# Layer 1's last denominators in two more even stretches, and layer 3's mean-times-scale moved from VectorE to GpSimd

## The chip, the cores and the metric

The kernel runs on one core of one Trainium2 chip. The metric is the device time of one execution in microseconds, as the median of several runs. Engines are named as in the profile: PE is TensorE's matmul, PEld its weight load, DVE is VectorE, ACT is ScalarE, POOL is GpSimd, SP is SyncE (here a queue that issues transfers).

## The reference

Four graph layers follow each other, each of the form `x = layernorm(x + layer(x, adj))`, on 2708 rows of 256 features with a 2708 x 2708 adjacency matrix. Two of them matter here.

```
# layer 1, per head of 4 (64 features each)
h    = (x @ W).reshape(n, heads, head_dim)
e    = leaky_relu(src[:, :, None] + dst.T[None, :, :])
attn = softmax(where(adj > 0, e, NEG_INF), axis=-1)
out  = einsum('nhm,mhd->nhd', attn, h)           # then a layer norm
# layer 3
h = features @ neigh_W.T
h = adj @ h / (adj.sum(axis=1) + 1)
z = concatenate([features, h], axis=-1) @ lin_W.T
out = layernorm(x + z)                           # (y - mean) * (var + eps) ** -0.5
```

In layer 1 the kernel never forms the softmax: it sums unnormalised weights times `h` (the sums), sums the weights themselves (the denominators), and divides at the end.

## The kernel before

The 2708 rows are 22 tiles of up to 128. In layer 1 the outputs are worked off in three groups of two spans of tiles: the spans are 4, 4, 4, 4, 3 and 3 tiles, so two groups have 512 + 512 output rows and the last has 384 + 276 = 660 (the last tile has 20 rows). For each group the loop runs over two pairs of heads (`q` of 0 and 1) and, within a pair, over the 22 source tiles (`c`). A turn of `c` does this:

- DVE makes two weight tiles `p`, one for each head of the pair, of 128 x 1024 or, in the last group, 128 x 660 (line 835). Five `p` buffers rotate.
- PE adds into the sums: `heads` (line 817) runs four matmuls, for each span (`cols`) and each of the two heads, with 64 columns of weights each. The two heads of one span stand in different columns of the array.
- PE adds into the denominators: `totals` (line 826) runs four matmuls, again for each span and head, with 32 columns of weights each. The four stand in four different column groups, number `2 * (s ^ q) + i`, and all write the one PSUM tile `den`.

`heads` and `totals` change their order from turn to turn, so two `totals` and then two `heads` stand together. Between turns, `step` puts in pieces of the group before: transposes of its sums and denominators (lines 694, 695), its normalisation on DVE, ACT and POOL (`layer1_end`, lines 671 to 744), and, with `q` of 1, the transposes and products of the next layer's logits (lines 756, 773). At the end of each `q`, ACT copies the sums (line 848) and the denominators (line 852) from PSUM into `dens`, one tile per span, which the next group's `layer1_end` transposes. The last group's `layer1_end` runs beside the start of layer 2.

In layer 3 the product `adj @ h` is formed with fewer products by the two halves of the rows (`seven`, line 328) in three units, whose results are turned back by PE (`rows3`, line 1387) tile by tile, and the two tiles of `last3`, numbers 19 and 20, get plain products of 22 matmuls (line 1428). The last unit's turning back stands between the matmuls of tiles 19 and 20. For every tile `row3` runs: DVE scales and adds the row part (line 1368), then `moments` takes mean and variance on DVE (lines 172, 174, 176) and raises to the power -0.5 on POOL (line 177). The rest of the normalisation is put off: `ended` holds the tile, and `flush`, called in the `row3` of the next tile behind its `moments`, works it off: DVE forms `-mean * rs` (line 1361), ACT applies scale and bias to the 128 x 256 tile (line 1362), and the tile is written out (line 1363) from the ACT queue where its number is odd, from SP where it is even. SP's queue also issues nearly all loads of the adjacency matrix. The order on each engine is set by a planner that places instructions, not by the order of the text: it puts line 1361 of a tile ahead of the next tile's line 1368 where it expects the power to be done.

After the last write the program ends in a conditional (line 1654) that skips the variant for signed inputs.

Of the kernel before, what the change touches and what calls it, by code (L numbers as in the profile page):

```python
# [14 lines left out]
AF = mybir.ActivationFunctionType  # L15
ALU = mybir.AluOpType
# [3 lines left out]
P = 128  # L20
# [7 lines left out]
def kernel(  # L28
# [24 lines left out]
    nc = tc.nc  # L53
# [9 lines left out]
    CT = 32  # L63
# [18 lines left out]
    last3 = [t for t in range(NT) if min(P, N - t * P) == P][-2:]  # L82
# [6 lines left out]
    def sz(i):  # L89
        return min(P, N - i * P)  # L90

    def width(lo, hi):
        return min(hi * P, N) - lo * P
# [110 lines left out]
    def load_strip(pool, t):  # L204
        s = pool.tile([P, NT, P], F32, tag="strip", name="strip", bufs=2)
        nc.sync.dma_start(s, adj_t[t])
        return s
# [28 lines left out]
    def gru_load(pool, bih, bhh):  # L236

        raw = pool.tile([P, 2, 3 * FC], F32, tag="braw", name="braw", bufs=2)
        for i, src in enumerate((bih, bhh)):
            nc.sync.dma_start(raw[:, i], src.rearrange("(c p) -> p c", p=P))  # L240
        return raw
# [162 lines left out]
    if True:  # L404
# [12 lines left out]
        if True:  # L417
            def load_fall(dst, g, queue):
                at, w = spans[g][0] * P, width(*spans[g])
                off = at - spans[g - g % 2][0] * P  # L420
                queue.dma_start(dst[:, :, off : off + w], bcast_rows(fall_d, at, w))
# [34 lines left out]
            with pool("l0", 2) as l0:  # L456
# [48 lines left out]
                with pool("prep", side="right") as prep:  # L505
# [24 lines left out]
                    with tc.issue_after(landed.ins):  # L530
# [9 lines left out]
                        bias = [gru_load(prep, *ab) for ab in ((e_bih, e_bhh), (n_bih, n_bhh))]  # L540
# [64 lines left out]
                    t = ahead + 1  # L605
                    s = load_strip(l0, t)
# [21 lines left out]
                for t in range(ahead + 2, NT - 1):  # L628
                    s = load_strip(l0, t)
# [7 lines left out]
                t = NT - 1  # L637
                s = load_strip(l0, t)
# [22 lines left out]
            if True:  # L661
# [123 lines left out]
                dens = [keepr.tile([P, W], F32, name=f"den{s}") for s in range(2)]  # L785
                for g in range(0, len(spans), 2):
                    segs = spans[g : g + 2]
                    at, w = segs[0][0] * P, width(segs[0][0], segs[-1][1])
                    if g >= 4:
                        falls.append(fallp.tile([P, H, 2 * W], F32, tag="fall_b", name="fall_b"))  # L790
                        for i in range(len(segs)):
                            load_fall(falls[-1], g + i, nc.sync)
                    cols = [(lo * P - at, width(lo, hi)) for lo, hi in segs]
                    sums, steps, halves = [], [itertools.chain(*rest)] if g == 0 else [], []

                    def step(c):
                        for s in list(steps):
                            if next(s, s) is s:
                                steps.remove(s)

                        if q == 0 and c % 5 == 1 and len(halves) < len(ended):
                            halves.append(layer1_end(l1, ended[len(halves)]))
                            next(halves[-1])
                            steps.append(itertools.islice(halves[-1], 2))

                        if q == 1 and c % 5 == 0 and c // 5 < len(halves):
                            steps.append(itertools.chain(halves[c // 5], [None], layer1_logits(ended[c // 5])))
                            next(steps[-1])

                    for q in range(H // 2):  # L810
                        den = ps_acc.tile([P, W], F32, tag="acc", name="den")
                        acc = [ps_acc.tile([P, W], F32, tag="acc", name="acc") for _ in segs]

                        def heads(c, ps, flags):
                            for s, (p0, ws) in enumerate(cols):
                                for i in (1, 0):
                                    nc.tensor.matmul(  # L817
                                        acc[s][i * HD : (i + 1) * HD, :ws], hs[c][:, 2 * q + i, :HD],
                                        ps[i][:, p0 : p0 + ws], **flags,
                                    )  # L820

                        def totals(c, ps, flags):
                            for s, (p0, ws) in enumerate(cols):
                                for i in (1, 0):
                                    j = (2 * (s ^ q) + i) * CT
                                    nc.tensor.matmul(  # L826
                                        den[j : j + CT, :ws], hs[c][:, 2 * q + i, HD + 1 - CT :],
                                        ps[i][:, p0 : p0 + ws], **flags,
                                    )

                        for c in range(NT):
                            ps = []
                            for i in range(2):
                                p = l1.tile([P, 2 * W], F32, tag="p", name="p", bufs=5)
                                nc.vector.scalar_tensor_tensor(  # L835
                                    p[:, :w], falls[g // 2][:, 2 * q + i, :w], rise[:, c, 2 * q + i : 2 * q + i + 1],
                                    mask[:, c, at : at + w], ALU.max, ALU.mult,
                                )
                                ps.append(p)

                            for part in (heads, totals)[:: -1 if c % 2 == 0 else 1]:
                                part(c, ps, dict(start=(c == 0), stop=(c == NT - 1)))
                                if part is (totals, heads)[c % 2]:
                                    step(c)
                        got = []
                        for s, (p0, ws) in enumerate(cols):
                            sb = keepr.tile([P, W], F32, tag=f"sum{q}{s}", name=f"sum{q}{s}")
                            nc.scalar.copy(sb[:, :ws], acc[s][:, :ws])  # L848
                            got.append(sb)
                        for s, (p0, ws) in enumerate(cols):  # L850
                            two = slice(2 * (s ^ q) * CT, 2 * ((s ^ q) + 1) * CT)
                            nc.scalar.copy(dens[s][two, :ws], den[two, :ws])
                        sums.append(got)
                    for a in steps:
                        for _ in a:
                            pass
                    ended = [(t, s, sums, dens, t - segs[0][0]) for s, (lo, hi) in enumerate(segs) for t in range(lo, hi)]
                    ended = [ended[i : i + 2] for i in range(0, len(ended), 2)]
# [24 lines left out]
                for i in range(SPLITS):  # L883
                    part = u_parts[:, :, i * K : (i + 1) * K]
# [7 lines left out]
                for t in range(NT):  # L892
                    for b, acc in zip(banks, pus):
                        w = width(*spans[b[0]])
# [56 lines left out]
                def band_tile(nm):  # L951
                    return tail.tile([P, NT, BANDS, K], F32, tag=nm, name=nm, bufs=1)
# [7 lines left out]
                d, q, keep_q = band_tile("d"), band_tile("q"), band_tile("keep_q")  # L960
# [6 lines left out]
                for i in range(SPLITS):  # L967
                    part = q_parts[:, :, i * B : (i + 1) * B].rearrange("p t (b k) -> p t b k", k=K)
# [8 lines left out]
                for g in range(0, len(spans), 2):  # L977
                    two, w = range(g, g + 2), width(*spans[g])
# [16 lines left out]
                shift, den = tail.tile([P, NT, K], F32, name="shift", bufs=1), tail.tile([P, NT, K], F32, name="den", bufs=1)  # L995
# [23 lines left out]
                for lo in range(0, NT, 4):  # L1019
                    hi = min(lo + 4, NT)  # L1020
                    at, w = lo * P, width(lo, hi)
                    pt = ps_t.tile([P, 4, P], F32, tag="tr", name="pst")
                    for t in range(lo, hi):
                        n = sz(t)
# [80 lines left out]
    with (  # L1105
# [250 lines left out]
        def flush():  # L1356

            while ended:
                t, o, mean, rs = ended.pop()
                n = sz(t)  # L1360
                nc.vector.scalar_tensor_tensor(mean, mean, -1.0, rs, ALU.mult, ALU.mult)  # L1361
                nc.scalar.activation(o[:n], o[:n], AF.Identity, scale=rs, bias=mean)  # L1362
                (nc.scalar if t % 2 else nc.sync).dma_start(out[t * P : t * P + n, :], o[:n])

        def row3(t, o, acc):
# [51 lines left out]
        for t, tag in zip(last3, ("m1", "m26")):  # L1417
            o = nleft.tile([P, F], F32, tag="y", name="y", bufs=3)
# [3 lines left out]
            for lo in range(0, NT, per):  # L1422
                hi = min(lo + per, NT)
                s = nright.tile([P, 2, 2, W], F32, tag="p", name="p", bufs=3).rearrange("p i h w -> p (i h w)")
                s = s[:, : (hi - lo) * P].rearrange("p (c n) -> p c n", n=P)
# [275 lines left out]
```

## Time and profile before

| | |
|---|---|
| median of 3 runs | 1865.03 us (1864.9 to 1866.25) |
| profiled execution, its own time | 1865.35 us |
| its span | 1863.6 us |
| PE busy | 1832.7 us (98%) |
| DVE busy | 1280.9 us (69%) |
| ACT busy | 699.3 us (38%) |
| POOL busy | 266.4 us (14%) |
| last group of layer 1 | 498.2 to 590.5 us |
| layer 3's last unit turned back, and its end | 1835.9 to 1856.5 us |

Times in the profile count from the start of the span. PE works nearly all the time, so a change is worth something where it shortens what PE does, where it takes away a wait of PE's, or behind PE's last matmul, where other engines finish alone. fp32 matmuls appear as two records each. Lines of the profile are lines of the kernel before.

### The profile page before, as it was taken

What the parts mean: (1) busy time and instruction counts of PE and PEld (TensorE: products, weight loads), DVE (VectorE), ACT (ScalarE), POOL (GpSimd) and SP (SyncE); (2) the same over time, 40 slices, a digit from 0 to 9 for tenths busy, and PEclk for the clock granted to TensorE, in tenths of its full rate; (3) what the DMA queues carried; (4) which work ended last, traced back from release to release, by engine and by line L of the source; (5) the groups of instructions that cost most, each with busy time, mean ns of one, the idle gap of its engine ahead of it and who ended that gap; (6) DMA issues with size and microseconds to landing.
All of it is one profiled execution on the core that took longest, in us unless ns stands there. A gap on an engine that the chain in (4) does not pass through costs nothing. (4 is left out here: it accounts for less than half of the span.)

```text
span 1863.6 us, 23088 instructions
## 1 busy us (share of the span) xinstructions
PE 1832.7 (98%) x7526; PEld 1035.4 (56%) x7530; DVE 1280.9 (69%) x2263; ACT 699.3 (38%) x1442; POOL 266.4 (14%) x427
## 2 busy tenths in 40 slices
PE   9999999999999999999999999999999999999997
PEld 7788832233345887887444444444445556654555
DVE  5344489999897664754568888776887768844664
ACT  3544410033144203111546655555665556321011
POOL 1211220001012411000002000111200302111111
PEclk9999999999999999999999999999999999999999
DMA  8344410100002667754647666454554545634764
GB/s 298 133 148 151 168 30 1 30 1 12 12 7 71 144 144 186 182 130 114 182 131 207 176 174 171 123 159 114 165 151 121 135 106 141 167 106 116 203 163 121
DMA packets 435101, 237.32 MB, mean 127 GB/s; under 512 B 184363, under 2 KB 422348, under 8 KB 432540
## 3 DMA queue, kind: packets, MB, share of 16 engines
q1 hardware_dynamic: 422414, 208.66, 41.4%
q0 software_dynamic: 8208, 22.59, 3.9%
q10 hardware_dynamic: 4350, 4.50, 0.7%
q8 instruction: 62, 1.02, 0.2%
q14 instruction: 67, 0.55, 0.1%
HBM read 223.00 MB, written 12.66 MB: 126 GB/s over the span
## 5 line engine op out<-in xcount | busy, mean ns | idle before, releaser
L835 DVE SCALAR_TENSOR_TENSOR p<-fall_b,rise,mask 128x1024 f32<-128x1024 f32 (+1 forms) x264 | 293.9, 1156 | 32.5 <-PE den L826 16.7
L1328 ACT ACTIVATE p<-st,e_neg 128x1024 f32<-128x1024 f32 (+1 forms) x198 | 197.3, 1040 | 193.9 <-PE m L328 190.1
L328 PE MATMUL m<-s,xq 128*128 128x512 f32 (+3 forms) x660 | 230.1, 467 | 0.0
L817 PE MATMUL acc<-p,h 128*64 128x512 f32 (+2 forms) x1056 | 214.5, 548 | 0.2 <-ACT sum L848 0.2
L328 PE MATMUL m<-p,xq 128*128 128x512 f32 (+1 forms) x396 | 183.0, 544 | 0.1
L215 PE MATMUL acc<-turn,strip 128*128 128x257 f32 x792 | 181.8, 379 | 0.0
L1331 ACT ACTIVATE p<-p 128x1024 f32<-128x1024 f32 (+1 forms) x198 | 178.8, 942 | 0.2
L315 DVE TENSOR_TENSOR s<-p 128x512 f32<-128x512 f32 (+3 forms) x132 | 81.5, 618 | 136.6 <-PE m L328 112.7
L328 PE MATMUL m<-p,x 128*128 128x512 f32 (+1 forms) x396 | 167.7, 542 | 0.3 <-DVE supt L345 0.3
L328 PEld LDWEIGHTS m<-s,xq 128*128 128x128 f32 x660 | 124.5, 190 | 76.3 <-issue 59.2
L1332 DVE TENSOR_TENSOR p<-p,blk 128x1024 f32<-128x1024 f32 (+1 forms) x132 | 142.8, 1101 | 33.6 <-ACT p L1331 23.1
L215 PEld LDWEIGHTS acc<-turn,strip 128*128 128x128 f32 x792 | 147.2, 190 | 20.3
L817 PEld LDWEIGHTS acc<-p,h 128*64 128x64 f32 x1056 | 69.8, 136 | 138.2 <-issue 128.6
L328 PE MATMUL m<-s,x 128*128 128x512 f32 (+3 forms) x330 | 127.2, 467 | 0.0
L826 PE MATMUL den<-p,h 128*32 128x512 f32 (+2 forms) x1056 | 117.8, 548 | 0.0
L328 PEld LDWEIGHTS m<-p,xq 128*128 128x128 f32 x396 | 74.6, 190 | 76.9 <-issue 61.3
L328 PEld LDWEIGHTS m<-p,x 128*128 128x128 f32 x396 | 74.8, 190 | 75.5 <-issue 61.1
L474 ACT ACTIVATE below<-strip 128x384 bf16<-128x384 f32 x132 | 78.4, 594 | 68.4 <-DMA strip<-in_adj_t_dram 65.0
L316 DVE TENSOR_TENSOR p<-p 128x512 f32<-128x512 f32 (+3 forms) x132 | 82.3, 624 | 2.3
L328 PEld LDWEIGHTS m<-s,x 128*128 128x128 f32 x330 | 62.0, 190 | 39.2 <-issue 34.6
L318 DVE TENSOR_TENSOR s<-p,s 128x512 f32<-128x512 f32 (+3 forms) x132 | 81.2, 615 | 1.9
L286 POOL TENSOR_TENSOR blk<-blk,offdiag 128x128 f32<-128x128 f32 (+3 forms) x50 | 28.2, 566 | 376.0 <-DMA blk<-in_adj_t_dram 359.2
(288 smaller groups left out, 2591.9 us busy)
## 6 DMA issues: line engine op xcount, KB each, us to landing
strip<-in_adj_t_dram SPq DMA_DIRECT2D x19, 1408.0 KB, 6.0
blk<-in_adj_t_dram SPq DMA_DIRECT2D x88, 256.0 KB, 3.4
blk<-in_adj_t_dram SPq DMA_DIRECT2D x88, 192.0 KB, 4.1
pa<-in_adj_t_dram SPq DMA_DIRECT2D x110, 128.0 KB, 2.8
turn<-in_adj_t_dram SPq DMA_DIRECT2D x44, 256.0 KB, 3.1
blk<-in_adj_t_dram SPq DMA_DIRECT2D x88, 128.0 KB, 2.7
p<-in_adj_t_dram SPq DMA_DIRECT2D x88, 128.0 KB, 2.7
turn<-in_adj_t_dram SPq DMA_DIRECT2D x44, 192.0 KB, 3.1
```

The source lines that it names most:

```text
L215: at = nc.tensor.matmul(acc, s[:, c, :n], rhs(c), start=(c == 0), stop=(c == NT - 1))
L315: nc.vector.tensor_tensor(s1, a21, a22, ALU.add)
L316: nc.vector.tensor_tensor(a21, a21, a11, ALU.subtract)
L318: nc.vector.tensor_tensor(s4, a12, s2, ALU.subtract)
L328: nc.tensor.matmul(dst[:, :w], lt, rt, start=start and not (one_bank and i), stop=stop and not (one_bank and i in (1, 2, 5)))
L474: nc.scalar.activation(below[:, : (hi - lo) * P], s[:, lo:hi].rearrange("p c n -> p (c n)"), AF.Relu, scale=-1.0, accum_out=negative[:, BE ...
L817: nc.tensor.matmul(acc[s][i * HD : (i + 1) * HD, :ws], hs[c][:, 2 * q + i, :HD], ps[i][:, p0 : p0 + ws], **flags,)
L826: nc.tensor.matmul(den[j : j + CT, :ws], hs[c][:, 2 * q + i, HD + 1 - CT :], ps[i][:, p0 : p0 + ws], **flags,)
L835: nc.vector.scalar_tensor_tensor(p[:, :w], falls[g // 2][:, 2 * q + i, :w], rise[:, c, 2 * q + i : 2 * q + i + 1], mask[:, c, at : at + w] ...
L1328: nc.scalar.activation(p[:, :, :w], st_k[:, :, :w], AF.Relu, scale=-1.0, bias=e_neg[:, at, k : k + 1])
L1331: nc.scalar.activation(p[:, :, :w], p[:, :, :w], AF.Exp, scale=-1.0)
L1332: nc.vector.tensor_tensor(p[:, :, :w], p[:, :, :w], blk[:, i, :, :w], ALU.mult)
```

## The change

In layer 1, the denominators of a group are no longer split at the border of its spans but at `cut`, the middle of the group's rows rounded to a multiple of 64 and not behind the border. A group of 1024 rows is still split 512 + 512. The last group's 660 rows are split 320 + 340, where it was 384 + 276. The copies into `dens` keep their targets: the first span's 384 rows now come from two column groups, 320 and 64 rows, the second span's 276 from one. So ACT makes three copies at the end of each `q` of the last group, where it made two. The sums keep the spans.

In layer 3, `-mean * rs` moves from DVE to POOL, as one tensor_scalar on the same 128 x 1 columns, and for tile 20, the last, both that and ACT's normalisation are replaced by one DVE instruction on the 128 x 256 tile.

```diff
                     cols = [(lo * P - at, width(lo, hi)) for lo, hi in segs]
+                    cut = min(cols[1][0], (w // 2 + P // 4) // (P // 2) * (P // 2))
+                    halves_at = [(0, cut), (cut, w - cut)]
...
                         def totals(c, ps, flags):
-                            for s, (p0, ws) in enumerate(cols):
+                            for s, (p0, ws) in enumerate(halves_at):
                                 for i in (1, 0):
                                     j = (2 * (s ^ q) + i) * CT
                                     nc.tensor.matmul(
...
                             two = slice(2 * (s ^ q) * CT, 2 * ((s ^ q) + 1) * CT)
-                            nc.scalar.copy(dens[s][two, :ws], den[two, :ws])
+                            for i, (a, n) in enumerate(halves_at):
+                                lo, hi = max(p0, a), min(p0 + ws, a + n)
+                                if lo < hi:
+                                    part = slice(2 * (i ^ q) * CT, 2 * ((i ^ q) + 1) * CT)
+                                    nc.scalar.copy(dens[s][two, lo - p0 : hi - p0], den[part, lo - a : hi - a])
...
                 t, o, mean, rs = ended.pop()
                 n = sz(t)
-                nc.vector.scalar_tensor_tensor(mean, mean, -1.0, rs, ALU.mult, ALU.mult)
-                nc.scalar.activation(o[:n], o[:n], AF.Identity, scale=rs, bias=mean)
+                if t == last3[-1]:
+                    nc.vector.tensor_scalar(o[:n], o[:n], mean, rs, ALU.subtract, ALU.mult)
+                else:
+                    nc.gpsimd.tensor_scalar(mean, mean, rs, -1.0, ALU.mult, ALU.mult)
+                    nc.scalar.activation(o[:n], o[:n], AF.Identity, scale=rs, bias=mean)
                 (nc.scalar if t % 2 else nc.sync).dma_start(out[t * P : t * P + n, :], o[:n])
```

The planner then orders anew. PE's order stays the same throughout. DVE's and ACT's order changes inside layer 1's last group, where some of `layer1_end`'s instructions move from the first `q` into the second, and in layer 3 from the first turned tiles on. On SP, three writes of finished tiles in layer 3 move ahead by one load each.

## The prediction

> **What bounds the kernel now.** I read the page first, for which engine is full; then busy time by stretches around the two edited places; then the timeline of PE in layer 1; last the timeline of the end.
>
> ```profile
> PE 1832.7 (98%) x7526; PEld 1035.4 (56%) x7530; DVE 1280.9 (69%) x2263; ACT 699.3 (38%) x1442; POOL 266.4 (14%) x427
> ```
>
> PE is busy for 1832.7 of 1863.6 us, so matmul time that is saved counts unless another engine takes over. The two `q` of layer 1's last group, by stretches (columns: length, then busy us and instructions of PE, PEld, DVE, ACT, POOL, then clock, DMA share, GB/s):
>
> ```profile
> 498.20:544.50 46.30, 46.07 (x388) 21.04 (x388) 44.55 (x86) 24.26 (x126) 6.61 (x7) 1.00 0.00 1
> 544.50:590.50 46.00, 46.00 (x386) 22.41 (x382) 35.82 (x49) 9.39 (x28) 8.60 (x19) 1.00 0.08 23
> ```
>
> PE is full in both. In the first `q` DVE is nearly full too, 44.55 of 46.3 us: the place where a faster PE could meet DVE. In the second DVE has 10 us to spare. Now PE's timeline (start, us, then the instruction; x16 is two turns of `c`), of a full group and of the last:
>
> ```profile
> 325.80 3.65 PE L817 MATMUL acc<-p,h 128*64 128x512 f32 x16
> 329.38 1.92 PE L826 MATMUL den<-p,h 128*32 128x512 f32 x16
> 331.24 3.65 PE L817 MATMUL acc<-p,h 128*64 128x512 f32 x16
> ...
> 523.37 2.44 PE L817 MATMUL acc<-p,h 128*64 128x384 f32 x16
> 525.74 1.49 PE L826 MATMUL den<-p,h 128*32 128x384 f32 x16
> 527.16 2.44 PE L817 MATMUL acc<-p,h 128*64 128x384 f32 x16
> ```
>
> From start to start, two turns of sums take 3.58 us for 512 + 512 rows and 2.37 for 384 + 276: they follow the total, 1.67 ns a row and turn. Two turns of denominators take 1.86 us with 512 and 512 and 1.42 with 384 and 276, a ratio of 0.763. The longer stretches stand as 0.75, the totals as 0.645. So the denominators follow the longer stretch. The end, in the timeline of all engines (the bracket is the idle time before, and what ended it):
>
> ```profile
> 1846.81 4.48 PE L1428 MATMUL m<-turn,p 128*128 128x256 f32 x20
> ...
> 1851.43 0.16 DVE L1361 SCALAR_TENSOR_TENSOR bn_mv<-bn_mv,bn_rs 128x1 f32<-128x1 f32 x1 [0.71 <-POOL bn_rs L177]
> 1851.52 0.47 DVE L1368 SCALAR_TENSOR_TENSOR o<-m,rdeg,o 20x256 f32<-20x256 f32 x1
> ...
> 1853.54 0.15 DVE L1361 SCALAR_TENSOR_TENSOR bn_mv<-bn_mv,bn_rs 20x1 f32<-20x1 f32 x1 [0.71 <-POOL bn_rs L177]
> 1853.62 0.47 DVE L1368 SCALAR_TENSOR_TENSOR y<-m,rdeg,y 128x256 f32<-128x256 f32 x1
> ...
> 1855.09 0.54 POOL L177 TENSOR_TENSOR bn_rs<-bn_rs,neg_half 128x1 f32<-128x1 f32 x1 [1.59 <-DVE bn_rs L176]
> 1855.67 0.16 DVE L1361 SCALAR_TENSOR_TENSOR bn_mv<-bn_mv,bn_rs 128x1 f32<-128x1 f32 x1 [0.72 <-POOL bn_rs L177]
> 1855.86 0.60 ACT L1362 ACTIVATE y<-y,bn_mv,bn_rs 128x256 f32<-128x256 f32 x1 [1.54 <-DVE bn_mv L1361]
> 1856.49 0.33 SPq L1363 DMA_DIRECT2D out_dram<-y  x1
> ```
>
> PE's last matmul ends at 1846.81 + 4.48 = 1851.29, but tile 20's line 1368 starts at 1853.62. DVE is late: line 1361 of each tile stands ahead of the next tile's line 1368 and waits 0.71 us for POOL. DVE's starts of line 1368 lie 2.15 us apart (1849.37, 1851.52, 1853.62), while PE turns a tile back every 1.52 us.
>
> **What the Trainium skill says.** "TensorEngine Tiling (Array Packing)", Key Properties: tiles work independently, and different ones can load weights and multiply in parallel. The 0.763 above agrees. "GPSIMD Engine Reference", section 3.1, has a two-input elementwise operation about twice as slow on GpSimd as on VectorE; the trace has no such multiply on one column, only the power, 0.54 us. "DMA: Bandwidth & Descriptors", Anatomy of one DMA, puts some 2 us of fixed cost on a transfer; the writes of line 1363 land after a median of 2.2 us, and nothing here changes that.
>
> **The change, part by part.**
>
> *Denominators on PE.* The longer stretch falls from 384 to 340 rows, for 44 turns (22 tiles, two `q`), 22 pairs. By the slope of the two measured pairs, (1.86 - 1.42) / 128 x 44 = 0.151 us a pair. But 340 and 320 are nearly even, like 512 and 512, whose pair has 0.147 us on top of its rows (1.854 - 4 x 512 x 0.000833 us, two passes a turn), against 0.134 with 384 and 276. With that a pair takes 1.133 + 0.147 = 1.280, a gain of 0.134. I take the lower one: 22 x 0.134 = **2.95 us**, at most 3.3.
>
> Does DVE keep up? It makes 44 tiles of 0.82 us a `q`, and the planner's new order takes work out of the first `q`: of lines 727 and 730 it leaves 9 there, where there were 13, at 0.41 and 0.47 us, some 1.75 us less. PE gives up 1.5 us in that `q`. So DVE falls with it, and the moved work finds 10 us of room in the second. PE waited little for `p` before and should stay so; if nothing of the first half's gain came through, 1.5 us would be lost.
>
> *The third copy on ACT.* Copies of 384 and 276 columns take 0.48 and 0.38 us. Three of 320, 64 and 276 take by their slope (0.10 / 108 columns) 0.42 + 0.20 + 0.38, so 0.15 more at the end of each `q`. At the first, PE waited for the copy of the sums, not for this. At the second, the transposes of line 695 wait for it and ACT is full (9.1 of 10 us from 590 to 600): I put 0.15 on the path, zero to 0.4 in the range.
>
> *From there to layer 3.* No engine's order changes, and loads start when PE gives buffers free, so they move with it. From 592 to 1830 PE idles for some 9 us in all, part of it for loads; I let the gain through whole, with 0.5 us of doubt.
>
> *Layer 3's multiply on POOL.* It leaves DVE: 22 records of 0.16 us, of which one goes without successor, and 10.6 us of waits for POOL, behind which the sums of `seven` (lines 315 to 318) and the next tile's line 1368 are queued. Amid matmuls PE covers most of that; weight loads waited 3.0 us for line 316, in five waits, and PE stood still for 1.75 us from 1700 to 1830. I take 0.2 us of gain, zero to 0.9. On POOL a tile now costs the power and one more operation. For that 0.32 us (twice DVE's 0.16, an estimate by the GPSIMD page) to 0.91 (the longest power, at 1727.90); I take 0.54. Both together, 1.1 to 1.45, stay under the 1.52 us between tiles, so POOL does not fall behind. ACT gets the scale about when it did; SP's writes, and the loads behind three of them that they are moved past, wait as long as before.
>
> *The end.* Without line 1361 a tile costs DVE 0.45 + 0.45 + 0.21 + 0.17 = 1.3 us, under PE's 1.52. DVE then follows PE: the 20-row tile's line 1368 starts near 1847.0, and its statistics end near 1848.3, so DVE is free when PE ends at 1851.29. Tile 20's line 1368 then starts at 1851.34, not 1853.62: **2.28 us**. From there to the power's end it takes 2.02 us as before. Behind it, 0.02 + 0.16 + 0.02 + 0.60 us of DVE and ACT become one DVE operation of 0.41 us (line 490, the same form) with its hand-over: 0.83 becomes 0.46, **0.35 us**. In all 2.63 us; the 7.1 us from the write's issue to the end stay.
>
> Sum: -2.95 + 0.15 - 0.2 - 2.63 = **-5.6 us**. The profiled execution of 1865.35 (span 1863.6, 1.75 around it) would become 1859.7. It lies 0.3 above the median of 1865.03, so the median becomes **1859.4 us**.
>
> **The rivals.**
>
> - *DVE or ACT takes over in layer 1* (chance 0.14). For it: 44.55 of 46.3 us. Against: the new order relieves that half. Half of 2.95 is lost: 1860.9, or 1861.9 with a late hand-over to layer 2.
> - *One half of the change brings nothing* (0.10). The denominators save nothing if the four column groups shared one stream of rows, since 660 stay 660; the ratio 0.763 speaks against. Or layer 2's loads hold the gain back. Then the end alone is left: 1865.03 - 2.8 = 1862.2.
> - *SP becomes the bound* (0.03), slower. A write waits on SP for ACT, which now waits for one more POOL operation, and loads of the matrix stand behind it. DVE's line 315 already waits 23.6 us for such loads in layer 3, in 12 waits. There are six writes amid loads; from 0.95 us of delay each, reaching PE, the whole 5.6 us are gone, and at 1.6 us each the time is 1865.03 + 6 x 1.6 - 5.6 = 1869. Against: the write waits for the same power, and no longer for line 1361's turn on DVE.
>
> **The numbers.** The likeliest case has 0.73 and gives 1859.4. Its own bounds are 1857.9 (slope 3.3, no copy, 0.9 in layer 3) to 1860.4. Rivals reach to 1862.2, so the range is 1857.9 to 1862.2. About 0.2%, 3.7 us, is what a measurement can tell here: faster means under 1861.3. The likeliest case and most of the first rival lie there: 0.85. Within 0.2%: 0.12. Slower: 0.03.
>
> **What would show it.** In the profile after, x16 of denominators in the last group take near 1.28 us from start to start, and the group ends near 588. Line 1361's waits for POOL are gone from DVE, PE's last matmul ends near 1848.3, tile 20's line 1368 starts within 0.1 us of that, and the write is issued 2.6 us behind it. Gaps of PE that DVE's `p` ends, in the first `q`, would make the first step wrong; a DVE still late at the last matmul, the last.

## The result, and the profile after

| | before | after |
|---|---|---|
| median of 8 runs each | 1865.68 us (1864.9 to 1867.76) | 1859.58 us (1857.93 to 1862.98) |
| profiled execution, its span | 1863.6 us | 1859.1 us |

The ratio is 0.9966, its 95% interval 0.9957 to 0.9975: 6.1 us less, 4.7 to 8.0 by the interval. The prediction was 1859.4 us. First the page's busy line of the kernel after:

```profile
PE 1831.6 (99%) x7530; PEld 1034.6 (56%) x7530; DVE 1277.7 (69%) x2242; ACT 700.0 (38%) x1443; POOL 273.6 (15%) x448
```

PE's busy time falls by 1.1 us only, though the denominators alone save 3. The reason is that single executions differ elsewhere: PE reaches layer 1's last group 1.85 us later after than before (498.45 instead of 496.60), and is busy 2.09 us longer up to there. The delay arises between 85 and 102 us, in layer 0, where the programs are alike. PE waits 1.93 us there for a copy of ACT's, instead of 1.23, and its next matmuls run slower: the four of line 429 take 2.07 us instead of 1.16. From 88 to 92 us the granted clock was 0.57 in this execution and 1.00 in that of before. So spans of two profiled executions are not compared below, but stages within them.

In lines of after, line 817 is 819, 826 is 828, 835 is 837, 852 is 858, 1368 is 1377 and 1428 is 1437; POOL's new multiply is line 1370 and the fused instruction for the last tile line 1368. The two `q` of layer 1's last group by stretches:

```profile
498.20:543.00 44.80, 44.80 (x393) 19.91 (x395) 41.62 (x76) 22.79 (x118) 5.92 (x5) 1.00 0.01 1
543.00:588.00 45.00, 45.00 (x388) 21.36 (x380) 38.85 (x61) 12.22 (x36) 10.47 (x20) 1.00 0.06 19
```

PE (the first busy time behind the length) is full in both, so what its matmuls save is saved. DVE (the third) falls from 44.55 of 46.3 us to 41.62 of 44.8 in the first and rises from 35.82 to 38.85 in the second, as work of `layer1_end` moves over. PE's timeline in the first `q`:

```profile
514.95 1.35 PE L828 MATMUL den<-p,h 128*32 128x320 f32 x16
516.23 2.44 PE L819 MATMUL acc<-p,h 128*64 128x384 f32 x16
518.60 1.35 PE L828 MATMUL den<-p,h 128*32 128x320 f32 x16
```

From start to start a pair of denominators takes 1.28 us, where it took 1.42; the sums stay at 2.37. The end, in the timeline of all engines:

```profile
1845.10 4.48 PE L1437 MATMUL m<-turn,p 128*128 128x256 f32 x20
1845.30 0.47 DVE L1377 SCALAR_TENSOR_TENSOR o<-m,rdeg,o 20x256 f32<-20x256 f32 x1
...
1849.62 0.49 DVE L1377 SCALAR_TENSOR_TENSOR y<-m,rdeg,y 128x256 f32<-128x256 f32 x1 [2.95 <-PE m L1437]
...
1851.19 0.55 POOL L177 TENSOR_TENSOR bn_rs<-bn_rs,neg_half 128x1 f32<-128x1 f32 x1 [3.48 <-DVE bn_rs L176]
1851.78 0.41 DVE L1368 TENSOR_SCALAR y<-y,bn_mv,bn_rs 128x256 f32<-128x256 f32 x1 [0.74 <-POOL bn_rs L177]
1852.22 0.33 SPq L1372 DMA_DIRECT2D out_dram<-y  x1
```

PE's last matmul ends at 1845.10 + 4.48 = 1849.58. DVE has then stood idle for 2.95 us and begins tile 20 at once, at 1849.62; before, it began 2.33 us behind PE. The write is issued 2.64 us behind PE's end, where it was 5.20.

Read in this way from the timelines, every kernel that ran can be cut into the same stages. S1 runs from the pair of denominators that holds the first turn of layer 1's last group (and the last turn of the group before) to the first transposes behind the last (line 694), the middle from there to the end of PE's last matmul, the end from there to the issue of the last write; in brackets, how far DVE's work on tile 20 starts behind PE's end. Ratios are to the kernel before, timed together with each; its median was 1865.28 us beside e1_den, e2_l3, e3_last and e7_behind, and 1865.44 us beside the other four.

| kernel | median us, ratio (interval) | S1 | middle | end |
|---|---|---|---|---|
| before | 1865.68 | 93.91 | 1260.78 | 5.20 (2.33) |
| after | 1859.58, 0.9966 (0.9957 to 0.9975) | 90.80 | 1260.32 | 2.64 (0.04) |
| e1_den | 1862.19, 0.9985 (0.9978 to 0.9991) | 90.80 | 1260.30 | 5.21 (2.33) |
| e2_l3 | 1862.56, 0.9986 (0.9979 to 0.9992) | 93.91 | 1261.05 | 2.64 (0.04) |
| e3_last | 1864.64, 0.9994 (0.9986 to 1.0003) | 93.91 | 1261.22 | 4.83 (2.33) |
| e4_pool | 1863.53, 0.9989 (0.9982 to 0.9995) | 93.91 | 1260.90 | 3.18 (0.04) |
| e7_behind | 1861.60, 0.9981 (0.9973 to 0.9990) | 93.91 | 1257.94 | 2.55 (0.04) |
| e5_cut256 | 1865.28, 0.9999 (0.9991 to 1.0008) | 96.24 | 1259.69 | 2.64 (0.04) |
| e6_cut330 | 1859.74, 0.9970 (0.9957 to 0.9983) | 90.41 | 1259.40 | 2.64 (0.04) |
| e9_both | 1858.40, 0.9961 (0.9948 to 0.9975) | 90.42 | 1259.38 | 2.55 (0.04) |

S1 is 93.91 in all five executions with the old split and 90.80 in both with the new one, and the end repeats as well. The middle varies by 3.3 us from one execution to the next. From before to after S1 gives -3.11, the end -2.56, together **-5.7 us**, where the medians give -6.1.

The middle hides a loss. PE's order is the same in all ten kernels, but for two weight loads that change places in e5_cut256, so their executions can be compared weight load by weight load (7530 in each). Most of the middle's spread goes with no kernel; e3_last alone, for one, loses 1.96 us to before between 1615 and 1625 us, where the two are alike. One place differs by kernel, near 1749 us of before: there PE loses 0.59 to 1.31 us against before in all five executions with the multiply on POOL (after: 0.78), while the four others with it on DVE differ from before by 0.02 at most. The instructions there before, and then after:

```profile
1746.35 0.61 DVE L315 TENSOR_TENSOR s<-p 128x430 f32<-128x430 f32 x1 [1.67 <-DMA p<-in_adj_t_dram]
1749.96 0.89 PE L328 MATMUL m<-p,hq 128*128 128x430 f32 x2
```

```profile
1747.79 0.61 DVE L315 TENSOR_TENSOR s<-p 128x430 f32<-128x430 f32 x1 [4.29 <-DMA p<-in_adj_t_dram]
1749.10 0.99 PE L328 MATMUL m<-p,hq 128*128 128x430 f32 x2 [0.52 <-DVE p L316]
```

DVE waits for a load of the matrix, and PE for DVE. The load is late because it is queued on SP behind the write of a finished tile, which waits for ACT's normalisation. From 1700 to 1756 us SP waits 3.8 us for ACT ahead of three such writes, where it waited 1.9 before; the five executions with POOL have 3.2 to 3.9, the five with DVE 0.8 to 1.9. Counted from the same place in PE's work, the loads behind the third write are issued 1.2 to 1.9 us later after than before. So with this loss the change gives -4.9 us by stages, still inside the interval of the medians. Two things come together in it, POOL's longer way to the scale and the planner's order, which puts the writes ahead of one more load; they were not run apart.

### The profile page after: what moved, and what is told of

Same layout as the page of the kernel before. It is cut to its first block, busy times and chain, and to the rows that moved or that the text cites. A ratio compares the mean times of both kernels' runs of the same rounds, so it can differ in the third digit from the quotient of the medians.

```text
span 1859.1 us, 23100 instructions
## 1 busy us (share of the span) xinstructions
PE 1831.6 (99%) x7530; PEld 1034.6 (56%) x7530; DVE 1277.7 (69%) x2242; ACT 700.0 (38%) x1443; POOL 273.6 (15%) x448
## 4 chain that ended last, share of the span: by engine, by line
PE 90%; DMA 4%; DVE 2%; SPq 1%; ACT 1%; issue 1%; POOL 0%; DVEq 0%; POOLq 0%; ACTq 0%
PE m L328 40%; PE acc L819 11%; PE acc L215 8%; PE bank L1193 7%; PE den L828 6%; PE gate L1068 4%; PE bank L1169 3%; PE bank L1236 2%; PE acc L521 2%; SPq L275 1%; PE pm L429 1%; PE m L1437 1%; DMA p<-in_adj_t_dram 1%; DVE p L1338 1%; DMA turn<-in_adj_t_dram 1%; DMA blk<-in_adj_t_dram 1%
```

## The experiments

**The halves apart.** e1_den is the new denominators with the old layer 3, e2_l3 the old denominators with the new layer 3. The kernel after with one half of its diff undone each:

```diff
 e1_den
-                if t == last3[-1]: ... else: nc.gpsimd.tensor_scalar(mean, mean, rs, -1.0, ALU.mult, ALU.mult) ...
+                nc.vector.scalar_tensor_tensor(mean, mean, -1.0, rs, ALU.mult, ALU.mult)
 e2_l3
-                            for s, (p0, ws) in enumerate(halves_at):
+                            for s, (p0, ws) in enumerate(cols):
```

> The denominators split 320 + 340 alone; layer 3 as before. Theory (the longest of the four stretches sets a pair of turns): a pair takes 1.28 us where it took 1.42, layer 1's last group gets 2.9 to 3.2 us shorter, from 93.9 us (first pair of the group to the transposes behind it) to about 90.8, the end stays at 5.2 us from PE's last matmul to the write's issue; time 2.9 us (0.16%) below the kernel before. Rival (the four share one stream of rows, and the gain came from elsewhere): pair and group as before, time unchanged. Rival (VectorE takes over in the first q): the group gains only about 1.5 us, with gaps of PE that end with line 835's successor.

> Layer 3's part alone: the multiply on GpSimd for all tiles but the last, the last normalised by VectorE; denominators 384 + 276 as before. Theory (VectorE was late at PE's last matmul because it waited for the power): the end shrinks from 5.2 to 2.6 us, layer 1's last group stays at 93.9; time 2.6 us (0.14%) below the kernel before, up to 3.5 if PE waits less in layer 3's units. Rival (the gain in layer 3 is in the units, where VectorE's line 315 to 318 no longer stand behind a wait): the end as before, 1 us or more gained between 1640 and 1830.

Against 1865.28 us of the kernel before, e1_den gave 1862.19 us (-3.1) and e2_l3 1862.56 us (-2.7). Each interval excludes 1, and the sum, -5.8, agrees with the -6.1 of the whole change. In the stages e1_den has S1 of after and the end of before, e2_l3 the reverse. So the halves add up, and neither brings nothing. The units of layer 3 gain nothing in e2_l3; near 1749 us it loses 0.67.

**The two parts of the end apart.** e3_last has only the fused instruction for the last tile and keeps the multiply of the others on DVE; e4_pool has the multiply on POOL for every tile, the last too, and no fused instruction:

```diff
 e3_last
+                if t == last3[-1]:
+                    nc.vector.tensor_scalar(o[:n], o[:n], mean, rs, ALU.subtract, ALU.mult)
+                else:
                     nc.vector.scalar_tensor_tensor(mean, mean, -1.0, rs, ALU.mult, ALU.mult)
 e4_pool
-                nc.vector.scalar_tensor_tensor(mean, mean, -1.0, rs, ALU.mult, ALU.mult)
+                nc.gpsimd.tensor_scalar(mean, mean, rs, -1.0, ALU.mult, ALU.mult)
```

> Of the whole change only the last tile: normalised by one VectorE instruction; the other tiles' multiply stays on VectorE, the denominators stay 384 + 276. Theory: the wait ahead of line 1368 stays, VectorE is still 2.3 us late at the last matmul, and only the hand-over at the very end is saved, 0.35 us: from 5.2 to about 4.85 us, time 0.35 us below before, not to be told from no change. Rival (the last tile's fusion carries the end's gain): 2.6 us between PE's last matmul and the write's issue.

> The multiply on GpSimd for every tile, the last too, which ACT normalises as before; denominators 384 + 276. Theory (two separate savings at the end, 2.3 us for VectorE's lateness and 0.3 to 0.4 us for the fused last tile): line 1368 of the last tile starts at once behind PE's last matmul; behind the power come the GpSimd multiply (0.27 us and its hand-over) and ACT's 0.60 us, so the write's issue is 3.2 us behind the last matmul, between the 2.64 of the changed kernel and the 5.2 of before. Rival (the two need each other): 2.6 or above 4.5.

e3_last gave 1864.64 us, a ratio whose interval holds 1, so its time alone decides nothing. Its end does: 4.83 us, 0.37 less than before, with DVE as late as before (2.33). e4_pool gave 0.9989, and its end is 3.18 us with DVE 0.04 behind PE. The last rows of its timeline:

```profile
1853.09 0.55 POOL L177 TENSOR_TENSOR bn_rs<-bn_rs,neg_half 128x1 f32<-128x1 f32 x1 [3.48 <-DVE bn_rs L176]
1853.73 0.26 POOL L1361 TENSOR_SCALAR bn_mv<-bn_mv,bn_rs 128x1 f32<-128x1 f32 x1
1854.03 0.60 ACT L1362 ACTIVATE y<-y,bn_mv,bn_rs 128x256 f32<-128x256 f32 x1 [3.79 <-POOL bn_mv L1361]
1854.66 0.33 SPq L1363 DMA_DIRECT2D out_dram<-y  x1
```

From the power's start to the write it is 1.57 us here, 1.40 before (1855.09 to 1856.49), and 1.03 after (1851.19 to 1852.22). So the wait that left DVE is worth 2.02 + 0.17 us at the end, of which POOL's longer multiply takes the 0.17 back at the last tile, and the fused instruction takes 0.54 off that chain, or 0.37 off the chain with DVE's multiply. Either way the two parts sum to 2.56.

**Is it POOL, or the place in the queue?** e7_behind leaves the multiply on DVE, but places it behind the next tile's line 1368 (there line 1372) instead of ahead of it. It also fuses the last tile, and leaves out one call of `flush` that has nothing left to do. `issue_after` sets the place of an instruction on its engine's queue:

```diff
+                if t == last3[-1]:
+                    nc.vector.tensor_scalar(o[:n], o[:n], mean, rs, ALU.subtract, ALU.mult)
+                else:
+                    with tc.issue_after(behind.ins) ...:
                         nc.vector.scalar_tensor_tensor(mean, mean, -1.0, rs, ALU.mult, ALU.mult)
...
-            nc.vector.scalar_tensor_tensor(o[:n], acc[:n, :F], rdeg[:n, t : t + 1], o[:n], ALU.mult, ALU.add)
+            at = nc.vector.scalar_tensor_tensor(o[:n], acc[:n, :F], rdeg[:n, t : t + 1], o[:n], ALU.mult, ALU.add)
             mean, rs = moments(o, n)
-            flush()
+            flush(at)
```

> Nothing goes to GpSimd: the multiply stays on VectorE, but is ordered behind the next tile's line 1368 (the 20-row tile's stays ahead of tile 20), and the last tile is normalised by VectorE; denominators 384 + 276 as before. Theory (it is the wait's place in VectorE's queue that counts, not VectorE's 0.16 us): VectorE keeps up with PE, some 1.5 us a tile, and the end is 2.6 us, as with the multiply on GpSimd. Rival (VectorE's work on the multiply matters, 0.16 us for each of ten tiles): the end lies between 2.6 and 5.2, near 4.

It gave 1861.6 us, a ratio of 0.9981, and the shortest end of these, 2.55 us. Two tiles of DVE's timeline and the last one:

```profile
1842.70 0.48 DVE L1372 SCALAR_TENSOR_TENSOR o<-m,rdeg,o 128x256 f32<-128x256 f32 x1
...
1843.48 0.16 DVE L1365 SCALAR_TENSOR_TENSOR bn_mv<-bn_mv,bn_rs 128x1 f32<-128x1 f32 x1 [0.29 <-POOL bn_rs L177]
...
1844.32 0.48 DVE L1372 SCALAR_TENSOR_TENSOR o<-bank,rdeg,o 128x256 f32<-128x256 f32 x1
...
1849.15 0.48 DVE L1372 SCALAR_TENSOR_TENSOR y<-m,rdeg,y 128x256 f32<-128x256 f32 x1 [0.71 <-PE m L1432]
```

The multiply still waits for POOL's power, but 0.3 us instead of 0.71, since most of the power's time now passes under line 1372. A tile costs DVE 1.62 us instead of 2.15, and at the last tile DVE waits for PE. So POOL isn't what gains; that the wait no longer stands in full ahead of the next tile's first instruction is. The way over POOL even costs something: e7_behind has no loss near 1749 us, where e2_l3 has 0.67. Its median is 1.0 us below that of e2_l3, of which this and the shorter end (0.09) account for 0.76, though the two intervals overlap.

**What sets the denominators' time.** All splits have 660 rows; only the longer stretch changes, 404 rows in e5_cut256 and 330 in e6_cut330:

```diff
 e5_cut256
-                    cut = min(cols[1][0], (w // 2 + P // 4) // (P // 2) * (P // 2))
+                    cut = min(cols[1][0], w // 2 // 256 * 256)
 e6_cut330
+                    cut = min(cols[1][0], w // 2)
```

> The whole change, but the denominators' border at 256: stretches of 256 and 404 rows, where the kernel before has 384 and 276. Theory (the longest stretch counts): a pair of turns takes 4 x 404 x 0.833 ns + 0.134 = 1.48 us against 1.42 before and 1.28 with 320 and 340, layer 1's last group 1.4 us longer than before, 95.3 us, though the copies and the order of the four matmuls are of the changed kernel's kind. Rival (any split of the four that differs from the sums' helps, for the order on the engines or the copies): the group near 91.

> The whole change, but the border in the exact middle, 330 and 330. Theory: a pair takes 4 x 330 x 0.833 ns + 0.147 = 1.25 us, 22 pairs gain another 0.7 us: the group takes 90.1 us, the time is 0.7 us below the changed kernel's, too little for the whole time to show. Rival (something else bounds the group by now, such as VectorE's weight tiles in the first q): the group stays at 90.8.

In e5_cut256 a pair takes 1.49 us (514.89 to 516.38), in e6_cut330 1.25 us. The pairs now known, by longer stretch: 1.86 (512), 1.49 (404), 1.42 (384), 1.28 (340), 1.25 (330). All of them are four passes of the longer stretch at 0.833 ns a row (half of the 1.67 ns that the sums take for a row and turn), plus 0.14 to 0.15 us; a shared stream of 660 rows would have left the last four equal.

But S1 was not what the pairs say, in either. e5_cut256 was to have 95.3 us and has 96.24. Of its turns from start to start of two pairs, all but two are as long as the pairs make them; two in the second `q` take 5.10 and 5.56 us, where before's 4.77 with 0.08 on top would be 4.85. They hold 0.25 + 0.71 = 0.96 us, as much as the excess. In both PE waits for ACT. PE's row of the second, and ACT's timeline beside it:

```profile
580.42 1.05 PE L773 MATMUL pm<-uw,turn 128*128 128x3 f32 x8 [0.64 <-ACT turn L758]
```

```profile
579.42 0.48 ACT L743 ACTIVATE o_mean<-o_mean,o_rs 128x1 f32<-128x1 f32 x2 [1.74 <-POOL o_rs L680]
579.80 0.56 ACT L758 COPY turn<-tr 128x512 f32<-128x512 f32 x1
```

PE's logits wait 0.64 us for the copy of line 758, and on ACT that copy is queued behind line 743, which had waited 1.74 us for POOL. In after's execution line 743 ran 8 us earlier, at 571.30, and its copy waited for PE alone. The planner had ordered the instructions anew for the new durations, so a change of a matmul's size cost 0.96 us through another engine's queue.

e6_cut330 was to save 0.7 us more than after in S1 and saved 0.39. Here the turns of the first `q` show it: 3.62 us as the pairs have it, but one of 3.77, and one of 4.54 where its like take 4.43, in all 0.26 us too long. In both DVE's `p` was late. The PE weight loads of the first, and PE's row:

```profile
517.89 0.20 PEld L819 LDWEIGHTS acc<-p,h 128*64 128x64 f32 x4 [0.42 <-DVE p L837]
```

```profile
516.63 2.59 PE L819 MATMUL acc<-p,h 128*64 128x384 f32 x16
```

The sums of this turn take 2.52 us from start to start (to 519.15) instead of 2.37. At three turns `p` is ready only 0.05 to 0.08 us ahead of PE; in after the smallest lead is 0.12, in before 0.11, and the same weight load of after waited 0.25 us with PE not held up. DVE's order is not quite that of after here, but counted from the start of S1 the late `p` is done only 0.03 us later. So between 340 and 330 rows DVE begins to take over in the first `q`.

**Both findings together.** e9_both has the split of e6_cut330, and layer 3 of e7_behind.

> Built from what the runs show: denominators 330 + 330, the multiply on VectorE behind the next tile's line 1368, the last tile normalised by VectorE. Theory: the group takes 90.1 us, the end 2.6 us; the time is 0.7 us below the changed kernel, 1859, and clearly below the kernel before, 0.35%. Rival (with the multiply back on VectorE the units of layer 3 lose): the stretch from layer 1's group to PE's last matmul is longer by more than 1 us than in the changed kernel.

It gave 1858.4 us, a ratio of 0.9961 to the kernel before, the lowest of all. Its stages are those of its parts: S1 90.42, end 2.55. Against the kernel after that is 0.47 us in these stages, and the 0.78 near 1749 us are gone as well: 1.25 in all, and 1.2 in the medians. The intervals of the two overlap, so the stages are the evidence, not the medians. The rival did not come: the middle is 0.94 us shorter than in the kernel after, not longer.

## Why the prediction was right, step by step

The forecast of 1859.4 us and the 1859.58 measured lie closer than the working earns. It started from 1865.03 us, where the larger count has 1865.68, and the change is 0.5 us larger than forecast. Several steps were off as well, in both directions.

- **Denominators on PE** (-2.95): right in mechanism and nearly in size. The pair was forecast at 1.28 and is 1.28 us; S1 gives -3.11. But only 21 of the 22 pairs gain 0.134 us, 2.81 in all. Where the two `q` meet, the stretches change column groups, so each group gets a long and a short one, and the pair takes 1.25 us in after, e5_cut256 and e6_cut330 alike. The other 0.30 us are luck: before, PE's sums behind this pair waited for ACT's copies of line 848. In the new order these copies start 0.35 us ahead of the pair instead of 1.04 behind its start, and the wait is gone. The rows before:

```profile
541.69 1.32 PE L826 MATMUL den<-p,h 128*32 128x384 f32 x16
543.24 2.44 PE L817 MATMUL acc<-p,h 128*64 128x384 f32 x16 [0.23 <-ACT sum L848]
```

  From the pair's start to the sums it is 1.55 us here, and 1.25 after (542.12 to 543.37).
- **DVE keeps up**: right at this cut, with as little to spare as before, as e6_cut330 shows. The rival that DVE takes over did not come at 340 rows, but it comes at 330. The rise of DVE in the second `q` found its room there.
- **The third copy on ACT** (+0.15): wrong in sign. The step took the sum of the three copies, 1.04 us instead of 0.88, as what the transposes of line 695 wait for. They wait for the first copy only, and that got shorter. ACT and PE at the end of the group, before:

```profile
590.51 0.77 PE L694 MATMUL tr<-ident,sum 128*128 128x128 f32 x5
590.66 0.88 ACT L852 COPY den<-den 64x384 f32<-64x384 f32 x2 [0.65 <-PE den L826]
591.19 0.20 PEld L695 LDWEIGHTS tr<-ident,den 128*128 128x128 f32 x2 [0.15 <-ACT den L852]
```

  and after:

```profile
589.26 0.77 PE L694 MATMUL tr<-ident,sum 128*128 128x128 f32 x5
589.37 1.04 ACT L858 COPY den<-den 64x320 f32<-64x320 f32 x3 [0.56 <-PE den L828]
589.86 0.42 PE L695 MATMUL tr<-ident,den 128*128 128x128 f32 x2
```

  Before, the first transposes of line 695 start 0.68 us behind those of line 694, with 0.15 us of waiting for the copy of 384 columns; after, 0.60 behind and with no wait, as the copy of 320 ends sooner. e1_den has the same 0.60. The work that hides the copy of 64 columns is this transposing of the first columns.
- **From there to layer 3, the gain let through whole**: right. e1_den's median of -3.1 is S1's -3.11, and compared weight load by weight load, the kernel after is 1.25 us ahead of before at the end of the group and 1.54 at 1700 us.
- **Layer 3's multiply off DVE** (-0.2 amid matmuls): wrong in sign. The 10.6 us of waits are gone from DVE, but PE had not been waiting for them. Instead weight loads wait 3.9 us for line 316 where they waited 3.0, and near 1749 us the kernel after loses 0.78 us. The step that failed is the one that had SP's writes, and the loads behind them, wait as long as before.
- **POOL's price for it** (0.54, with bounds of 0.32 and 0.91): mis-sized. The median of line 1370 is 0.27 us, below the low bound, which had come from the Trainium skill, "GPSIMD Engine Reference", section 3.1: about twice DVE's time. That section measured an addition of two tensors of 2048 columns; here it is another instruction on one column, 0.27 to 0.16, 1.7 times. POOL itself keeps up, with 1.5 us a tile.
- **SP as the bound**: came in small, at one of its places. SP's writes wait longer for ACT, and DVE's line 315 waits 29.1 us for loads where it waited 23.6. Of this 0.78 us reach PE, not the 5.6 that would have used up the gain; e2_l3, with the same writes, is faster than before.
- **The end** (-2.63: 2.28 of lateness, 0.35 of hand-over): right. Measured are 2.29 (2.33 to 0.04) and, by e3_last, 0.37, which is also what the forecast's own 0.83 and 0.46 give. Between them 0.10 us are lost: from the start of line 1368 to POOL's power it takes 1.57 us, where it took 1.47, which was forecast to stay. In all 2.56. DVE follows PE's 1.52 us a tile. The end of PE's last matmul was forecast near 1848.3 and came at 1849.58: this execution had entered the last group 1.85 us late, and S1 and the middle were 0.57 us shorter together than forecast.
- **The range**: its lower bound, from a slope of 3.3 us, no copy and 0.9 us in layer 3, comes to 1858.2 us by these figures, not 1857.9. Nothing depends on it.

## What to carry to other kernels

Where concurrent column groups of PE have unequal stretches, even them out: here a pair costs its longest stretch. But check the lead of the engine that feeds them, since here 0.12 us of it was all there was, and look at the other engines' new queue order before the size of the gain is believed. A short instruction that waits for another engine costs, in a queue worked in order, what is late behind it. Putting it behind the next tile's first instruction gave as much at the end as giving it to another engine, and spared the loss of 0.6 to 1.3 us that the latter had elsewhere: what finishes later may hold up a write, and the write the loads queued behind it. Cut profiled executions into stages at fixed instructions, since their spans differ by as much as what is sought; where PE's order is the same, compare them instruction by instruction.

## What was not expected of the hardware

- POOL's multiply of one column takes 0.27 us where its power on the same column takes 0.55: at the same size, the kind of instruction makes a factor of two.
- Executions of the same instructions in layer 0 differ: those of after and e1_den reach the last group 1.85 and 3.0 us later than before's, with a granted clock of 0.97 against 1.00 between 50 and 100 us. In after, the 17.09 us from 84.99 us on took 14.83 before (from 85.38 us): 0.70 of the difference are the longer wait, 1.56 the slower matmuls behind it. Why the clock fell there was not tested.
- The middle stage varies between 1257.9 and 1261.2 us among the kernels run. The loss near 1749 us is part of it; the rest goes with no kernel that ran, and its cause stays open.
